# A four-layer convolution and state-space network on one core: the state recurrence of layers 0 and 3 laid out as 8 channels by 16 states per partition block

## The chip, the cores and the metric

The kernel runs on one core of one Trainium2 chip. The metric is the device time of one execution, in microseconds (us); the time before is 17534.35 us, the median of three runs (17520.38 to 17538.02). All data is float32. The engines are TensorE (PE; its weight loads are PEld), VectorE (DVE), ScalarE (ACT), GpSimd (POOL) and SyncE (SP), which issues the transfers.

## The reference, cut to what matters

The input is 4 images of 64 channels by 64 by 64 pixels. Four layers follow one another. Layers 0 and 3 treat an image as a sequence of 4096 tokens and contain a selective state-space recurrence over 128 inner channels with 16 states each:

```
dA  = jnp.exp(dt[..., None] * A)                  # A is (128, 16)
dBx = dt[..., None] * Bm[:, :, None, :] * xc[..., None]
def step(hc, inp):
    dA_t, dBx_t, C_t = inp
    hc = hc * dA_t + dBx_t
    y = jnp.einsum('bds,bs->bd', hc, C_t)
    return (hc, y)
ys = (ys + xc * Dp) * jax.nn.silu(z)
```

dt, xc and z (per channel) and Bm, Cm (per state, the same for all channels) come from projections, a short convolution, silu and softplus. Layer 0 has 3 by 1, 1 by 3 and 1 by 1 convolutions, a ReLU and a layer norm ahead of this and a residual sum behind it; in layer 0 the state starts anew with each image. Layer 3 has a projection, a layer norm, silu and a residual sum behind it, and its state runs on through all four images. Layers 1 and 2 (a selective scan along both image axes, and a 3 by 3 filter with predicted weights) are not changed.

## The kernel before, in words

`Net.__init__` runs setup, then `mambas` for layer 0 of image 0 (tiles named `a`), and for each image layer 1 (`b`), layer 2 (`c`) and a `mambas` call that does layer 3 of this image (`d`) and layer 0 of the next (`a`). Each `mambas` call is a row of **jobs**: an image's 4096 tokens are 8 chunks of 512 tokens, one job each. There are 64 jobs in all, 32 of layer 0 and 32 of layer 3.

Within a job the 128 partitions are the 128 inner channels, and the state index is the loop: `scan` (L401) takes the 16 states in 8 pairs, and each tile of a pair is 128 by 2 by 512. For pair i:

- `spread` (L392) broadcasts two rows of B, and two of C, over the 128 partitions: four matmuls with 32 rows each (a column of the identity as the weights), in four different row blocks of the array, into the PSUM tiles bc0 and bc1 (two banks each).
- `decay` (L405): two ACT exponentials (L408) read dt (`dl`, in SBUF) and make the factors `a`.
- DVE multiplies bc0 by `wx` = dt times xc into `g` (L419, 1024 columns), runs two recurrences of 512 columns (L430, factors `a`, terms `g`, both in SBUF) into `h`, and multiplies bc1 by `h` into `o` (L436, 1024 columns).
- POOL copies the last column of `h` to the state (L433).
- `sums`: two matmuls with the 128 by 128 identity add `o` into the PSUM tile `y`; one more adds D times xc.

The projections and pointwise steps that prepare the next job (`mamba_front`, L455; for layer 0 also `cross`, `relu`, `square`, `norm`, `scaled`, from L584 on) and finish the last one (`out1`, `out2`, ... of `layer0` and `layer3`) are lists of small functions, each with a place. `mambas` sorts them into 17 places, two for each pair, and `scan` calls them between its own instructions. `in_order` (L97) then ties each engine to the order in which the program was written, so an instruction that waits holds up everything written behind it on its engine. On DVE the pieces of a place stand between `g` and the recurrences, or between the recurrences and `o`.

[...] `ps` is shared by all matmuls of `mamba_front`.

Of the kernel before, what the change touches and what calls it, by code (L numbers as in the profile page):

```python
# [10 lines left out]
F32 = mybir.dt.float32  # L11
# [27 lines left out]
SPARE = 512 - UC  # L39

# [14 lines left out]
class Net:  # L55
# [67 lines left out]
    def setup(self, sp, pp):  # L123
# [39 lines left out]

        self.mean64 = self.ctile([C, C], "mean64")
# [30 lines left out]
    def setup_mamba(self, sp, pp, n):  # L195
# [10 lines left out]
        for k in range(4):  # L206
# [15 lines left out]
        m["x4"] = x4 = self.ctile([DIN, 4, 32], f"{n}_x4")  # L222
        nc.vector.memset(x4, 0.0)
        nc.vector.tensor_copy(
            x4[:, :, 0 : NST // 2].rearrange("p (x t) j -> p x t j", t=2),
            xbc.rearrange("p (x j t) -> p x t j", x=2, t=2),
# [124 lines left out]
    def mambas(self, n, b0, b3, x3):  # L351

        nc, tc = self.nc, self.tc
        with ExitStack() as ctx:
            p = {}
            for k, bufs in (("w", 1), ("s", 2), ("n", 2)):
                p[k] = ctx.enter_context(tc.tile_pool(name=f"{n}_{k}", bufs=bufs))
            p["ps"] = ctx.enter_context(tc.tile_pool(name=f"{n}_ps", bufs=1, space=PSUM))
            jobs = self.layer3(b3, x3, p) if b3 is not None else []
            if b0 < NB:  # L360
                jobs += self.layer0(b0, p)
            for job in jobs[0:2]:
                for at, f in job["front"]:
                    if job is jobs[0] or at < 0:
                        f()
            last = {"seen": nc.cur_bb.bb.instructions[-1].name}
            sums = before = None
            self.spread(p, jobs[0], 0, 0)
            for job, after, later in zip(jobs, jobs[1:] + [None], jobs[2:] + [None, None]):
                places = [[] for _ in range(17)]  # L370
                for at, f in after["front"] if after else ():
                    if at >= 0:
                        places[at].append(f)
                for at, f in later["front"] if later else ():
                    if at < 0:
                        places[16 + at].append(f)
                for at, f in before["post"] if before else ():
                    late = before["m"] is self.m3 and after is not None and after["m"] is self.m0
                    places[at + 5 if late and at > 1 else at].append(f)
                sums = self.scan(p, job, after, places, sums, last)  # L380
                before = job
            sums()
            for _, f in before["post"]:
                f()
            if b3 is not None and b0 == NB:
                return
            self.x1 = jobs[-1]["x1"]()

    def spread(self, p, job, x, i):


        ps = p["ps"].tile([DIN, 2, TOK], F32, name=f"{job['n']}_bc{x}{i}", tag=f"bc{x}")  # L392
        for t in range(2):
            r = 64 * x + 32 * t
            pick = self.ident[r : r + 32, r + i : r + i + 1].to_broadcast([32, DIN])
            self.mm(ps[:, t, :], pick, job["bc"][r : r + 32])
        job["ps", x] = ps

    def scan(self, p, job, after, places, sums, last):
        nc, m, n = self.nc, job["m"], job["n"]  # L400
        xc, dl, wx = job["xc"], job["dl"], job["wx"]  # L401
        wide = wx.unsqueeze(1).to_broadcast([DIN, 2, TOK])

        def decay(i):
            a = p["n"].tile([DIN, 2, TOK], F32, name=f"{n}_a{i}", tag="a")  # L405
            for t in range(2):
                j = 2 * i + t
                nc.scalar.activation(a[:, t, :], dl, AF.Exp, scale=m["A"][:, j : j + 1])  # L408
            return a

        a = decay(0)
        for i in range(NST // 2):
            T = lambda tag: p["n"].tile([DIN, 2, TOK], F32, name=f"{n}_{tag}{i}", tag=tag)
            if sums:
                sums()
            if i == 2:
                self.mm(job["y"], m["D"], xc, False, False)
            g, h, o = T("g"), T("h"), T("o")
            nc.vector.tensor_tensor(g, job["ps", 0], wide, ALU.mult)  # L419
            if i + 1 < NST // 2:  # L420
                self.spread(p, job, 0, i + 1)
            elif after:
                self.spread(p, after, 0, 0)
            self.spread(p, job, 1, i)
            now, a = a, decay(i + 1) if i + 1 < NST // 2 else None
            for f in places[2 * i]:
                f()
            for t in range(2):
                st = m["state"][:, 2 * i + t : 2 * i + t + 1]
                nc.vector.tensor_tensor_scan(  # L430
                    h[:, t, :], now[:, t, :], g[:, t, :], st, ALU.mult, ALU.add
                )
            nc.gpsimd.tensor_copy(m["state"][:, 2 * i : 2 * i + 2], h[:, :, TOK - 1])  # L433
            for f in places[2 * i + 1]:
                f()
            nc.vector.tensor_tensor(o, job["ps", 1], h, ALU.mult)  # L436

            def sums(i=i, o=o):

                if i == 0:  # L440
                    job["y"] = p["ps"].tile([DIN, TOK], F32, name=f"{n}_y", tag="y")
                for t in range(2):
                    j = 2 * i + t
                    self.mm(job["y"], self.ident, o[:, t, :], j == 0, j == NST - 1)

            if i == NST // 2 - 1:
                for f in places[16]:
                    f()
            self.in_order(last)
        return sums  # L450

    def mamba_front(self, p, job, src, at):
# [49 lines left out]
        def rows():  # L502
            pr = P("pr")
            self.mm(pr, m["x4"].rearrange("p r j -> p (r j)"), job["xc"])
            job["bc"] = S("bc")
            nc.scalar.copy(job["bc"], pr)
# [12 lines left out]
        def soft4():  # L519
# [7 lines left out]
            zip(at, (conv, conv_out, gate, silu1, silu2, silu3, soft1, rows, soft2, soft3, soft4))  # L527
# [25 lines left out]
    def layer0(self, b, p):  # L553
# [19 lines left out]
        def chunk(c):  # L573
# [8 lines left out]
            def cross(part):  # L582
                def f():
                    if part == 0:  # L584
                        t["px"] = P("px", "ps")
# [21 lines left out]
            def scaled():  # L607
# [7 lines left out]
                (-4, cross(0)), (-2, cross(1)), (0, cross(2)), (0, relu), (1, square), (2, root),  # L615
                (3, newton), (3, scaled),
            ] + self.mamba_front(
                p, job, lambda k: hn[:, t0 + k : t0 + k + TOK], (4, 5, 6, 6, 9, 11, 12, 12, 14, 15, 16)
            )
# [19 lines left out]
            job["post"] = [(1, out1), (2, out2), (3, out3)]  # L639
# [4 lines left out]
    def layer3(self, b, x3, p):  # L644
        nc = self.nc

        def chunk(c):
# [7 lines left out]
                p, job, lambda k: x3[:, t0 + k : t0 + k + TOK], (2, 3, 4, 4, 7, 9, 10, 10, 12, 13, 14)  # L655
# [33 lines left out]
            def silu3():  # L689
# [10 lines left out]
                (1, out1), (2, out2), (3, square), (4, mean),  # L700
                *self.norm(p, n, t, self.l3_pb, None, (5, 7)),
                (7, silu1), (9, silu2), (11, silu3),
# [596 lines left out]
def _layout(i):  # L1299
# [12 lines left out]
    def mamba(n, g, conv_w, conv_b, D):  # L1312
        a[f"{n}_v128"] = c(conv_w, conv_b, g("dt_proj_b"), D, g("A_log"))
# [57 lines left out]
```

## Time and profile before

| | |
|---|---|
| median of three runs | 17534.35 us |
| the profiled execution's own time | 17525.53 us |
| its span, first to last instruction | 17523.8 us |
| mean granted TensorE clock | 0.968 |
| busy: PE / DVE / ACT / POOL | 94% / 92% / 71% / 40% |
| the five `mambas` stretches, by DVE's first and last tile of them | 447, 871, 864, 867, 453 us (3501 us in all) |
| the four layer 1 stretches | 3376 to 3379 us each |
| the four layer 2 stretches | 71 to 72 us each |

The times are in the order of the program, so a change to layers 0 and 3 is read from the five `mambas` stretches, a fifth of the span, and not from the busy shares of the whole, which layer 1 sets. In a group line the columns are source line, engine, operation, output and inputs, shapes and count, then busy time in us and mean ns of one instruction, then idle time of the engine just ahead of it and what ended it. A float32 matmul is recorded as two passes, so a count of 4 stands for two matmuls. Busy time of one group is what no other instruction of the engine covered.

### The profile page before, as it was taken

To read this page: it belongs to the slowest core of one execution; us is meant where nothing else is said; L and a number is where in the kernel's file an instruction comes from. 1 tells how busy PE (TensorE), PEld (TensorE's weight loads), DVE (VectorE), ACT (ScalarE), POOL (GpSimd) and SP (SyncE) were. 2 spreads that over 40 slices of the span, in tenths; PEclk is the share of its full clock that TensorE was granted. 3 is DMA by queue.
4 is the path that set the end of the run, shared out by engine and by line. 5 is a ranking of instruction groups with operands and counts; after the bars stand their busy time and mean duration, and the time that the engine had idled before them with its cause. 6 is when DMAs were issued, how large, how long until landed. Compare 5 with 4: busy or idle time off the path is not lost.

```text
span 17523.8 us, 606527 instructions
## 1 busy us (share of the span) xinstructions
PE 16417.9 (94%) x259788; PEld 10917.5 (62%) x259788; DVE 16093.1 (92%) x18426; ACT 12452.9 (71%) x15787; POOL 7093.0 (40%) x7068
## 2 busy tenths in 40 slices
PE   7999999997899999999779999999977999999997
PEld 2677777762267777776226777777622777777762
DVE  8999999988899999998899999999888999999978
ACT  4688878874468877886447887888644788788864
POOL 0444544441044444445114444444501444444440
PEclk9999999998999999999899999999988999999998
DMA  0233333330033333333003333333200333333320
GB/s 8 76 95 96 96 88 96 94 84 5 1 79 96 96 92 92 95 94 80 5 1 85 96 96 89 94 95 95 75 4 2 90 96 94 89 95 96 96 69 3
DMA packets 580492, 1281.87 MB, mean 73 GB/s; under 512 B 164664, under 2 KB 182304, under 8 KB 577824
## 3 DMA queue, kind: packets, MB, share of 16 engines
q1 hardware_dynamic: 577824, 1243.06, 28.1%
q8 instruction: 2069, 33.90, 0.9%
q14 instruction: 599, 4.91, 0.1%
HBM read 6.64 MB, written 4.19 MB: 1 GB/s over the span
## 4 chain that ended last, share of the span: by engine, by line
PE 85%; DVE 10%; ACT 2%; issue 2%; POOL 0%; DVEq 0%; DMA 0%; SPq 0%; POOLq 0%; ACTq 0%
PE b_u_S L120 24%; PE b_y L120 23%; PE b_z L120 23%; PE b_X L120 5%; PE d_y L120 2%; DVE a_h L430 2%; PE a_y L120 2%; DVE d_h L430 2%; DVE d_o L436 1%; DVE a_o L436 1%; PE c_p L120 1%; PE d_bc L120 1%; DVE a_g L419 1%; PE a_bc L120 1%; PE d_pc L120 1%
## 5 line engine op out<-in xcount | busy, mean ns | idle before, releaser
L1046 ACT ACTIVATE b_k_e<-b_z,shift 128x768 f32<-128x768 f32 x6144 | 5545.3, 903 | 2524.4 <-PE b_z L120 1408.7
L1126 DVE TENSOR_TENSOR b_k_r<-b_u_S,b_k_r 128x768 f32<-128x768 f32 x6144 | 5873.8, 956 | 462.3 <-PE b_u_S L120 110.9
L1101 DVE TENSOR_TENSOR b_k_e<-b_k_e,b_wt 128x768 f32<-128x768 f32 x6144 | 6221.5, 1013 | 29.3 <-ACT b_k_e L1046 29.3
L1046 ACT ACTIVATE b_k_r<-b_z,ln_eps 128x768 f32<-128x768 f32 x6144 | 5505.1, 896 | 0.0
L120 PE MATMUL b_u_S<-b_k_e,b_k_tB 64*64 64x192 f32 x98304 | 5169.8, 325 | 9.3 <-issue 4.3
L120 PEld LDWEIGHTS b_y<-b_k_r,b_k_dC 64*64 64x64 f32 x98304 | 3769.8, 133 | 2246.4 <-issue 2030.8
L120 PE MATMUL b_y<-b_k_r,b_k_dC 64*64 64x192 f32 x98304 | 5123.9, 322 | 36.5 <-DVE b_k_r L1126 36.5
L120 PE MATMUL b_z<-A,b_T 48*64 48x384 f32 x49152 | 5111.8, 485 | 11.6 <-ACT b_k_r L1046 7.9
L1075 POOL TENSOR_TENSOR b_k_tB<-b_BC,tri 128x512 f32<-128x512 f32 x3072 | 3259.7, 1061 | 4086.8 <-PE b_u_S L120 3827.2
L1075 POOL TENSOR_TENSOR b_k_dC<-b_BC,ident 128x512 f32<-128x512 f32 x3072 | 3227.7, 1051 | 2894.2 <-PE b_u_S L120 2015.8
L120 PEld LDWEIGHTS b_u_S<-b_k_e,b_k_tB 64*64 64x64 f32 x98304 | 3670.7, 133 | 581.9 <-issue 229.8
L120 PEld LDWEIGHTS b_z<-A,b_T 48*64 48x64 f32 x49152 | 1867.0, 134 | 203.9 <-ACT b_k_r L1046 48.8
L120 PE MATMUL d_y<-d_o,ident 128*128 128x512 f32 x1024 | 648.8, 767 | 416.3 <-DVE d_o L436 415.9
L120 PE MATMUL a_y<-a_o,ident 128*128 128x512 f32 x1024 | 583.5, 698 | 223.6 <-DVE a_o L436 221.9
L433 POOL COPY l_state<-d_h 128x2 f32<-128x2 f32 x256 | 119.0, 465 | 1625.5 <-DVE d_h L430 1625.5
L120 PEld LDWEIGHTS d_y<-d_o,ident 128*128 128x128 f32 x1024 | 212.3, 230 | 811.8 <-DVE d_o L436 617.6
L433 POOL COPY l_state<-a_h 128x2 f32<-128x2 f32 x256 | 110.5, 432 | 1425.5 <-DVE a_h L430 1425.5
L430 DVE TENSOR_TENSOR_SCAN a_h<-a_a,l_state,a_g 128x512 f32<-128x512 f32 x512 | 629.4, 1271 | 29.8 <-ACT a_u L497 0.5
L430 DVE TENSOR_TENSOR_SCAN d_h<-d_a,l_state,d_g 128x512 f32<-128x512 f32 x512 | 629.0, 1269 | 26.9 <-DVE d_g L419 1.4
L408 ACT ACTIVATE d_a<-d_dl,l_A 128x512 f32<-128x512 f32 x512 | 339.2, 711 | 354.5 <-DVE d_dl L522 183.2
L408 ACT ACTIVATE a_a<-a_dl,l_A 128x512 f32<-128x512 f32 x512 | 336.0, 709 | 318.4 <-DVE a_h L430 159.9
L120 PEld LDWEIGHTS a_y<-a_o,ident 128*128 128x128 f32 x1024 | 192.3, 208 | 593.1 <-DVE a_o L436 375.6
(352 smaller groups left out, 9914.4 us busy)
## 6 DMA issues: line engine op xcount, KB each, us to landing
b_k_r<-b_k_r SPq DMA_DIRECT2D x6144, 192.0 KB, 3.0
b_xs<-x SPq DMA_DIRECT2D x128, 67.0 KB, 2.7
b_xs<-x SPq DMA_DIRECT2D x128, 66.8 KB, 2.3
b_BC<-b_BC SPq DMA_DIRECT2D x512, 12.0 KB, 2.1
xin<-in_x SPq DMA_DIRECT2D x16, 256.0 KB, 5.8
out<-d_so SPq DMA_DIRECT2D x32, 128.0 KB, 2.3
l1w_cw<-in_l1w_cw SPq DMA_DIRECT2D x1, 384.0 KB, 3.4
l1h_cw<-in_l1h_cw SPq DMA_DIRECT2D x1, 384.0 KB
```

Source lines behind the costliest of these rows:

```text
L120: self.nc.tensor.matmul(out, lhsT=lhsT, rhs=rhs, start=start, stop=stop)
L408: nc.scalar.activation(a[:, t, :], dl, AF.Exp, scale=m["A"][:, j : j + 1])
L419: nc.vector.tensor_tensor(g, job["ps", 0], wide, ALU.mult)
L430: nc.vector.tensor_tensor_scan(h[:, t, :], now[:, t, :], g[:, t, :], st, ALU.mult, ALU.add)
L433: nc.gpsimd.tensor_copy(m["state"][:, 2 * i : 2 * i + 2], h[:, :, TOK - 1])
L436: nc.vector.tensor_tensor(o, job["ps", 1], h, ALU.mult)
L1046: nc.scalar.activation(o.rearrange("p x (j c) -> p j x c", j=2), zin, AF.Sigmoid, bias=bias, scale=scale)
L1075: nc.gpsimd.tensor_tensor(out, m.unsqueeze(3).to_broadcast(shape), x.unsqueeze(1).unsqueeze(2).to_broadcast(shape), ALU.mult,)
L1101: nc.vector.tensor_tensor(e, e, chunks[q]["w"][:, i, :].unsqueeze(1).unsqueeze(2).to_broadcast([128, 2, 2, D1]), ALU.mult,)
L1126: nc.vector.tensor_tensor(r, S.pop(k)[:, :, 0:UC], r, ALU.mult)
```

## The change: what it does

The layout of the recurrence is turned. A **group** is now 8 channels by 16 states on the 128 partitions, and a job is 16 groups (`NG`) of 512 columns, one recurrence each.

- B and C are made for all 128 partitions once in each job: `rows(0)` and `rows(1)` multiply xc by weights `wbc` in which the 16 columns are repeated 8 times, and ACT copies the results to SBUF tiles `bc0` and `bc1`.
- `decay`: a matmul with 32 rows (`pick`) spreads the 8 channels of dt that belong to the group over 128 partitions, into one PSUM bank `pe`; ACT takes the exponential from PSUM, with a scale for each partition, into `a` (5 buffers). It runs 4 groups ahead (`EXPS`).
- `wide`: the same for `wx`, into a PSUM tile `g` with 3 buffers, 3 groups ahead (`WXS`).
- `drive`: DVE multiplies `g` by `bc0` in place, in PSUM, one group ahead of the recurrence.
- `state`: the recurrence, terms from PSUM.
- `weigh`: after each second group POOL copies the last columns to the state and multiplies the pair's `h` (128 by 1024, 3 buffers) by `bc1`, in place, in SBUF.
- `sums`: two matmuls of 128 rows and 32 columns each (`gather`) sum the pair's states, each into another block of 32 partitions of `y`, one pair after `weigh`. D times xc now starts `y`.
- The pieces of the jobs beside it get 16 places, one for each group (`AT`); the layer 0 pieces `cross` to `scaled` move from places -4 to 3 to places -8 to -2. `px` moves from `ps` to the bank of `pv`. PSUM is `pe` 1, `g` 3, `y`, `ps`, `pl`, `pv` 1 each.
- Setup makes `gather`, `of32` and `wbc`; each `mambas` call makes `pick` with one DVE copy. The load of `v128` has the same size, with A permuted.

The core of the diff:

```diff
+GS = 8
+NG = DIN // GS
+EXPS, WXS = 4, 3
+AT = -1, 0, 1, 1, 4, 5, 6, 7, 7, 8, 9, 10
...
+            for j in range(EXPS):
+                self.decay(p, *steps[j])
+            for j in range(WXS):
+                self.wide(p, *steps[j])
+            self.drive(*steps[0])
...
+                for f in places[k]:
+                    f()
+                if j + 1 < len(steps):
+                    self.drive(*steps[j + 1])
+                self.state(p, job, k)
+                if j + EXPS < len(steps):
+                    self.decay(p, *steps[j + EXPS])
+                if j + WXS < len(steps):
+                    self.wide(p, *steps[j + WXS])
+                if k % 2:
+                    self.weigh(job, k - 1)
+                    if j > 2:
+                        self.sums(p, *steps[j - 3])
+                self.in_order(last)
...
+    def spread(self, p, out, x, k):
+        r = slice(32 * (k % 4), 32 * (k % 4) + 32)
+        self.mm(out, p["pick"][r, k // 4].rearrange("p c n -> p (c n)"), x[r])
+
+    def decay(self, p, job, k):
+        n = f"{job['n']}_{k}"
+        ps = p["ps"].tile([DIN, TOK], F32, name=f"{n}_pe", tag="pe")
+        self.spread(p, ps, job["dl"], k)
+        a = job["a", k] = p["n"].tile([DIN, TOK], F32, name=f"{n}_a", tag="a", bufs=EXPS + 1)
+        self.nc.scalar.activation(a, ps, AF.Exp, scale=job["m"]["A"][:, k : k + 1])
+
+    def drive(self, job, k):
+        g = job["g", k]
+        self.nc.vector.tensor_tensor(g, job["bc", 0], g, ALU.mult)
+
+    def state(self, p, job, k):
...
+        self.nc.vector.tensor_tensor_scan(
+            h[:, t, :], job.pop(("a", k)), job.pop(("g", k)), m["state"][:, k : k + 1],
+            ALU.mult, ALU.add,
+        )
+
+    def weigh(self, job, k):
+        nc, h = self.nc, job["h", k]
+        nc.gpsimd.tensor_copy(job["m"]["state"][:, k : k + 2], h[:, :, TOK - 1])
+        nc.gpsimd.tensor_tensor(
+            h, job["bc", 1].unsqueeze(1).to_broadcast([DIN, 2, TOK]), h, ALU.mult
+        )
+
+    def sums(self, p, job, k):
+        if k == 0:
+            job["y"] = p["ps"].tile([DIN, TOK], F32, name=f"{job['n']}_y", tag="y")
+            self.mm(job["y"], job["m"]["D"], job["xc"], True, False)
+        h = job.pop(("h", k))
         for t in range(2):
+            q, g = (k + t) % 4, (k + t) // 4
+            self.mm(
+                job["y"][32 * q : 32 * q + 32], self.gather[:, g, :], h[:, t, :], False, g == 3
+            )
...
-                (-4, cross(0)), (-2, cross(1)), (0, cross(2)), (0, relu), (1, square), (2, root),
-                (3, newton), (3, scaled),
+                (-8, cross(0)), (-7, cross(1)), (-6, cross(2)), (-6, relu), (-5, square), (-4, root),
+                (-3, newton), (-2, scaled),
```

## The prediction

> **What bounds it now.** The page's first part gives shares of the whole span:
>
> ```profile
> PE 16417.9 (94%) x259788; PEld 10917.5 (62%) x259788; DVE 16093.1 (92%) x18426; ACT 12452.9 (71%) x15787; POOL 7093.0 (40%) x7068
> ```
>
> Layer 1 makes these. The change lives in the `mambas` stretches, so I cut three pieces there, from one `yz` (the end of a job) to a later one: 6 layer 0 jobs of the first stretch, 7 layer 3 jobs, 7 layer 0 jobs behind them.
>
> ```profile
> core 0: us, PE busy (x) PEld busy (x) DVE busy (x) ACT busy (x) POOL busy (x), PEclk, DMA share, GB/s
> 143.00:452.40 309.40, 246.96 (x758) 76.24 (x758) 285.12 (x272) 146.94 (x216) 33.11 (x57) 0.96 0.00 0
> 4058.40:4437.50 379.10, 282.77 (x843) 88.82 (x844) 337.38 (x326) 187.06 (x279) 35.39 (x63) 0.88 0.01 3
> 4437.50:4814.30 376.80, 306.58 (x890) 92.14 (x888) 335.19 (x321) 177.35 (x261) 38.11 (x67) 0.91 0.00 1
> ```
>
> A job takes 309.4/6 = 51.6, 379.1/7 = 54.2 and 376.8/7 = 53.8 us. With the later stretches cut the same way the means are 53.0 (layer 0) and 54.2 (layer 3). DVE is busy 89 to 92%: it is the bound, and ACT (50%) and POOL (10%) are nearly free. PE is second, 75 to 81% busy. The groups say what DVE does, and the two c rows are used below:
>
> ```profile
> L430 DVE TENSOR_TENSOR_SCAN d_h<-d_a,l_state,d_g 128x512 f32<-128x512 f32 x512 | 629.0, 1269 | 26.9 <-DVE d_g L419 1.4 <-ACT d_dv L496 0.5
> ...
> L408 ACT ACTIVATE d_a<-d_dl,l_A 128x512 f32<-128x512 f32 x512 | 339.2, 711 | 354.5 <-DVE d_dl L522 183.2 <-DVE d_h L430 171.3
> ...
> L436 DVE TENSOR_TENSOR d_o<-d_bc,d_h 128x1024 f32<-128x1024 f32 x256 | 311.6, 1217 | 136.2 <-PE d_bc L120 132.7
> ...
> L419 DVE TENSOR_TENSOR d_g<-d_bc,d_wx 128x1024 f32<-128x1024 f32 x256 | 310.3, 1212 | 0.4
> ...
> L1279 POOL TENSOR_TENSOR c_acc<-c_acc,c_m 128x512 f32<-128x512 f32 x128 | 162.2, 1267 | 123.0 <-DVE c_m L1277 111.3 <-DVE c_st L1247 3.5
> ...
> L1277 DVE TENSOR_TENSOR c_m<-c_pk,x 128x512 f32<-128x512 f32 x144 | 97.0, 680 | 30.3 <-POOL c_acc L1279 14.4 <-POOL x L1283 7.9 <-PE c_pk L120 6.4
> ```
>
> The 132.7 us before `d_o` are DVE waiting for the C rows: PE reaches them late. The order of PE in one layer 3 job shows why:
>
> ```profile
> 4237.29 1.98 PE L120 MATMUL d_y<-d_o,ident 128*128 128x512 f32 x4
> 4239.20 1.14 PE L120 MATMUL d_bc<-d_bc,ident 32*128 32x512 f32 x8
> 4245.54 3.78 PE L120 MATMUL d_y<-d_o,ident 128*128 128x512 f32 x4 [5.20 <-DVE d_o L436]
> ```
>
> Two full matmuls take 1.98 us; four of 32 rows, in different row blocks, 1.14 together. After 5.2 us of waiting the same two take 3.78: the granted clock is halved (mean 0.88 in that window).
>
> **DVE's sum.** In the DVE timeline of that job a pair takes 1.14 (`o`, start to next start) + 1.35 (`g`, and the gap to the recurrence that depends on it) + 2.46 (two recurrences) = 4.95 us, eight times 39.6. The change removes `o` (1.14) and `g` (1.35) and adds two `drive`s of 512 columns. No row writes PSUM from DVE; the nearest (L1277, PSUM times SBUF) lasts 0.68 and starts every 0.60 when free, the dearest 512-column row is 0.74 (L549). I take 0.60, as each `drive` stands one group ahead of its recurrence and the gap goes. The recurrence with its terms in PSUM is not shown either; from SBUF it is 1.23 in a row of two, and the 1024-column rows cost the same from PSUM as from SBUF, so I keep 1.23. A group is 1.83, a job 16 x 1.83 = 29.3. The pieces beside it stay on DVE: 10.0 us in layer 0 (two of 1024 columns, 1.22 and 1.20; eleven of 512 at about 0.69), 10.7 in layer 3. DVE's floor is 39.3 and 40.0 us, against 39.6 + 10 or 10.7 before: 10.3 us freed in each job. What is late next takes half back.
>
> **The product on POOL.** 1024 columns cost between 2 x 1.05 (L1075, 512 columns, both inputs repeated) and 2 x 1.27 (L1279): I take 2.4, plus 0.2 to 0.45 for the state copy, eight times 22 us of a job: it fits. But POOL and DVE get in each other's way. First DVE, then POOL, in one stretch of layer 2:
>
> ```profile
> 8281.93 0.23 DVE L1243 TENSOR_TENSOR c_wl<-c_p,l_b 128x72 f32<-128x72 f32 x1 [0.69 <-PE c_p L120]
> ...
> 8283.50 0.77 DVE L1248 TENSOR_TENSOR c_wl<-c_wl,c_st 128x72 f32<-128x72 f32 x1
> ```
>
> ```profile
> 8282.91 2.62 POOL L1279 TENSOR_TENSOR c_acc<-c_acc,c_m 128x512 f32<-128x512 f32 x2 [0.25 <-DVE c_st L1247]
> ```
>
> 72 columns take 0.23 with an input from PSUM and 0.77 with both in SBUF, ending where POOL's first product ends. `c_m` (one input from PSUM) is not held. So `drive` should run free, and the pieces with both inputs in SBUF wait for a running product. A product starts behind each odd group and lasts until 2.9 us after its recurrence (0.1 + 0.4 + 2.4). An even group with no such piece takes DVE 1.83, so a piece that opens the next odd place waits 1.1: places 5 and 9. At place 10 four such pieces in a row let the copy and then the product in between: 0.2 + 2.4. Layer 0's norm pays 0.4 more. Sum: 5.2 us (layer 0), 4.8 (layer 3).
>
> The recurrence keeps one SBUF stream, `a`. The trace has no recurrence beside a POOL product for longer than 0.08 us (then 1284 ns against 1270), so its cost lies between 0 and 2.4 us a pair; I take 0, by `c_m`.
>
> [...]
>
> **PE.** Before, a pair costs 1.91 + 1.07 (start to next start) = 2.98. After: four spreads, two at a time in different row blocks, and two sums in different column blocks. Nothing shows sums of 32 columns; between side by side (1.07, as `d_bc`) and in turn (1.91, as `d_y`) I take 1.07, because the 64 by 64 blocks of layer 1 also run four at a time. That is 3.1 to 3.2 a pair, 43 us a layer 0 job with 17.7 of pieces, 36 in layer 3: below DVE, but with little room. PE is in order: `decay`'s spread waits until ACT has read the single bank `pe`, and the `wide` that the next `drive` needs is queued behind it. `wide` leads by one group beyond the one in hand, so the four matmuls of `conv` (3.63 us) at place 15 hold `drive` up by about 2.5. The sums wait for POOL, with 3.7 us and a spread to hide its 2.9: nothing.
>
> **ACT.** An exponential from PSUM is 0.69 (as L468, 687 ns), and spread and exponential alternate: about 1.9 a group, hidden by four groups of lead. But `silu3` (place 5) to `soft2` (place 7) is 1.2 of matmul, five ACT pieces of 0.64, and two exponentials: 5.8 us, where DVE has two groups, 3.7. DVE waits 2.0. Before, the same pieces stood three half pairs apart (7.4 us) and were covered.
>
> **Sum.** Layer 0: 39.3 + 5.2 + 2.5 + 2.0 = 49.0 against 53.0. Layer 3: 40.0 + 4.8 + 2.5 + 2.0 = 49.3 against 54.2. 32 x (4.0 + 4.9) = 285 us saved. Each of five stretches starts dearer: the first `wide` stands behind four spreads and three exponentials in turn, about 7 us, and setup adds 3: 38. Transfers are unchanged. 285 - 38 = 247 off the profiled execution's 17525.5 is 17278; the median lies 9 above it: **17287 us**, with 17120 to 17440 by the bounds of these costs.
>
> **Rivals**, from the same median.
> - Covers hold: POOL and DVE interleave well and the lead hides `conv` and the silu chain; jobs of 44.5. 32 x (8.5 + 9.7) - 38 = 544: **16990**. For it: the pieces wait only if they meet a product. Against: PE's 43 us.
> - The sums run in turn: 8 x 0.86 = 6.9 more on PE, 50 us a layer 0 job, 53 with the waits, 50 in layer 3: 32 x (0 + 4.2) - 38 = 96: **17440**; lower clocks would make it no change.
> - **Slower: the recurrence can't run beside POOL's product.** Place: the two recurrences of each pair; price 2.4 a pair: 8 x (3.66 + 2.4) + 10 = 58.5 and 59.2. 32 x (5.5 + 5.0) + 38 = 374: **17910**. It decides from about 1.1 us of waiting a pair. For it: `a` and the state come from SBUF. Against: `c_m`.
>
> **Chances.** Forecast 0.50; covers hold 0.18; sums in turn 0.17 (half of it below 17440, a third of it within 0.2% of no change, a little slower); recurrence held 0.12; else 0.03. A measurement of this kernel tells 0.2% (35 us) from no change. Faster 0.77, same 0.07, slower 0.16. The range, 16970 to 17580, takes in all but the held recurrence and the best covers.
>
> **What would show it.** Right: no `o` on DVE, `drive` near 0.68 and recurrence near 1.27; products of 2.4 on POOL; `silu3`, `soft3` and `soft4` two to four times as long as before; DVE waiting for PE before `drive` around place 15; sums starting within 0.1 us of each other. Wrong: recurrences beyond 1.5 us, products beyond 3, PE's clock below 0.85, or DVE waiting for ACT's factors at most groups.

## The result, and the profile after

The changed kernel takes **18906.56 us** (median of 4 runs, 18904.84 to 18912.01) against 17532.79 beside it: ratio **1.0785**, 95% interval 1.0766 to 1.0804. The prediction was 17287 with a range up to 17580, so it was wrong in sign and by 1620 us. The profiled execution took 18907.0 (span 18905.3).

All of it lies in the five `mambas` stretches: together 3501 us before and 4922 now, cut by DVE's first and last instruction in each (46 us of the growth is only that this first instruction now stands earlier). Layer 1 (3379 us a time) and layer 2 (71) are as they were. A layer 3 job takes 71.6 us instead of 54.2 (82 to 87 where its neighbours belong to layer 0), a layer 0 job mostly 74 to 79 instead of 53.

Of the page of the changed kernel, the engines' line and the rows of PE and of its clock:

```profile
PE 18224.0 (96%) x259916; PEld 11069.6 (59%) x259916; DVE 15720.0 (83%) x18436; ACT 12481.3 (66%) x15851; POOL 8275.7 (44%) x7580
...
PE   8999999999999999999999999999999999999998
...
PEclk7799999985589999998558999999855899999985
```

DVE's busy time fell by 373 us, as the change meant it to. PE's rose by 1806 with 128 more instructions among 260 thousand, so each one got longer; and where the stretches lie, the clock row says 5 to 8 tenths while the PE row says 9. The windows, cut from one `yz` to a later one, of five layer 0 jobs of the first stretch, five layer 3 jobs, and two layer 0 jobs behind them:

```profile
core 0: us, PE busy (x) PEld busy (x) DVE busy (x) ACT busy (x) POOL busy (x), PEclk, DMA share, GB/s
188.90:574.30 385.40, 363.20 (x650) 83.73 (x650) 208.24 (x225) 125.36 (x186) 119.05 (x88) 0.60 0.00 0
4280.30:4641.30 361.00, 330.94 (x590) 75.65 (x590) 211.33 (x231) 133.77 (x202) 119.13 (x85) 0.57 0.01 2
4977.20:5134.90 157.70, 150.57 (x260) 34.45 (x260) 83.42 (x91) 50.47 (x76) 46.01 (x34) 0.56 0.00 0
```

PE is the bound: 92 to 95% busy at a mean clock of 0.56 to 0.60 (before 0.88 to 0.96 at 75 to 81%). DVE is 53 to 59% busy. The trace records the granted clock as either full or half (1.0 in half of the entries and 0.5 in the others: 352 before, 218 now), in stretches that are multiples of 3.413 us; of the five `mambas` stretches, 776 of 3501 us were at half before, 4110 of 4922 are now. The record begins only 98.8 us into the span before and 140.7 us after. The matmuls of 512 columns ahead of that last 1.06 us in the median, as at half clock (0.59 and more at full), so some 49 and 106 us of the first stretch are missing from these two sums.

The groups of the layer 3 window show that the durations of single instructions on DVE, ACT and POOL are close to what the prediction took:

```profile
L124 PE MATMUL d_pe<-d_dl,d_pick 32*128 32x512 f32 x161 | 152.0, 1040 | 23.7 <-ACT d_a L442 23.7
L124 PE MATMUL d_g<-d_wx,d_pick 32*128 32x512 f32 x160 | 151.7, 1045 | 2.2 <-DVE d_h L460 2.2
L460 DVE TENSOR_TENSOR_SCAN d_h<-d_a,l_state,d_g 128x512 f32<-128x512 f32 x80 | 101.7, 1272 | 0.0
L469 POOL TENSOR_TENSOR d_h<-d_bc,d_h 128x1024 f32<-128x1024 f32 x40 | 96.0, 2399 | 3.3 <-POOL l_state L468 0.2
L124 PE MATMUL d_y<-d_h,gather 128*32 128x512 f32 x162 | 72.3, 988 | 0.0
L453 DVE TENSOR_TENSOR d_g<-d_bc,d_g 128x512 f32<-128x512 f32 x81 | 55.6, 687 | 66.6 <-PE d_g L124 66.6
L442 ACT ACTIVATE d_a<-d_pe,l_A 128x512 f32<-128x512 f32 x81 | 55.5, 685 | 206.3 <-PE d_g L124 189.7 <-PE d_pe L124 16.6
```

`drive` (L453) lasts 687 ns, the recurrence (L460) 1272, the product on POOL (L469) 2399. But `drive` waited 66.6 us for PE, the exponential (L442) 206. In the timeline of one job:

```profile
4336.12 7.19 PE L124 MATMUL d_pc<-x,l_wk 64*128 64x512 f32 x8
...
4343.24 1.22 PE L124 MATMUL d_pe<-d_dl,d_pick 32*128 32x512 f32 x1
...
4343.25 1.22 PE L124 MATMUL d_g<-d_wx,d_pick 32*128 32x512 f32 x1
...
4345.24 1.92 PE L124 MATMUL d_y<-d_h,gather 128*32 128x512 f32 x4
...
4345.39 0.70 DVE L453 TENSOR_TENSOR d_g<-d_bc,d_g 128x512 f32<-128x512 f32 x1 [7.25 <-PE d_g L124]
```

The four matmuls of `conv` take 7.19 us (3.70 at full clock before, 3.63 to the next start). One `decay` and one `wide` spread run together, from 4343.24 to 4345.24; two sums side by side take 1.92 (1.05 where the clock is full). A pair of groups has two such couples of spreads and one of sums: 2 x 2.0 + 1.86 = 5.86 us, eight times 46.9. In the third window above, added up from each matmul's start to the next (1.3 us at most for one), the spreads and sums of a layer 0 job take 48.7 us, the matmuls of its pieces 27.4, and the other 2.7 of its 78.8 us are waiting.

### The profile page after: what moved, and what is told of

It reads as the page before. It is cut to its first block, busy times and chain, and to the rows that moved or that the text cites. A ratio compares the mean times of both kernels' runs of the same rounds, so it can differ in the third digit from the quotient of the medians.

```text
span 18905.3 us, 607797 instructions
## 1 busy us (share of the span) xinstructions
PE 18224.0 (96%) x259916; PEld 11069.6 (59%) x259916; DVE 15720.0 (83%) x18436; ACT 12481.3 (66%) x15851; POOL 8275.7 (44%) x7580
## 5 line engine op out<-in xcount | busy, mean ns | idle before, releaser
L442 ACT ACTIVATE a_a<-a_pe,l_A 128x512 f32<-128x512 f32 x512 | 351.2, 686 | 1410.7 <-PE a_g L124 1151.2
L442 ACT ACTIVATE d_a<-d_pe,l_A 128x512 f32<-128x512 f32 x512 | 350.7, 685 | 1336.8 <-PE d_g L124 1180.1
L124 PE MATMUL d_pe<-d_dl,d_pick 32*128 32x512 f32 x1024 | 965.5, 1040 | 156.5 <-ACT d_a L442 156.5
L124 PE MATMUL d_g<-d_wx,d_pick 32*128 32x512 f32 x1024 | 956.1, 1047 | 12.1 <-DVE d_h L460 12.1
L124 PE MATMUL a_pe<-a_dl,d_pick 32*128 32x512 f32 x768 | 709.4, 1019 | 63.7 <-ACT a_a L442 63.7
L468 POOL COPY l_state<-a_h 128x2 f32<-128x2 f32 x256 | 63.5, 248 | 1609.5 <-DVE a_h L460 1552.5
L124 PEld LDWEIGHTS d_pe<-d_dl,d_pick 32*128 32x128 f32 x1024 | 233.9, 282 | 891.6 <-ACT d_a L442 418.5
L453 DVE TENSOR_TENSOR d_g<-d_bc,d_g 128x512 f32<-128x512 f32 x512 | 351.1, 687 | 466.8 <-PE d_g L124 466.8
L453 DVE TENSOR_TENSOR a_g<-a_bc,a_g 128x512 f32<-128x512 f32 x512 | 351.1, 686 | 463.6 <-PE a_g L124 463.4
```

The costliest lines, as they stand in the source:

```text
L124: self.nc.tensor.matmul(out, lhsT=lhsT, rhs=rhs, start=start, stop=stop)
L442: self.nc.scalar.activation(a, ps, AF.Exp, scale=job["m"]["A"][:, k : k + 1])
L453: self.nc.vector.tensor_tensor(g, job["bc", 0], g, ALU.mult)
L468: nc.gpsimd.tensor_copy(job["m"]["state"][:, k : k + 2], h[:, :, TOK - 1])
```

## The experiments

The theories. **A**: PE's clock is halved because the new matmuls use too little of the array. **B**: POOL's product holds up DVE. **P**: PE works in the order of the program (`in_order`), and the single bank of `decay` with what is queued behind it stops it. Most variants were run once, with a profile, beside one to seven runs of the kernel before on the same chip (medians 17511.7 to 17528.8); variants run four times spread over 2 to 25 us. Half clock means the sum over the five stretches in the trace's record. There are 64 jobs, 32 of each layer, and some of the expectations multiply by half of that: in the run with useless products 27 us a job make 1728 us, not 860; the waits for POOL's product that the prediction priced (the expectations call them locks) are 320 us in all, not 160; and the sums for the product on DVE and for the last two runs double as well. The order is that of the argument.

**POOL's product left out.**
```
-            h, job["bc", 1].unsqueeze(1).to_broadcast([DIN, 2, TOK]), h, ALU.mult
+            h[:, :, 0:1], job["bc", 1][:, 0:1].unsqueeze(1).to_broadcast([DIN, 2, 1]),
+            h[:, :, 0:1], ALU.mult
```

> This kernel leaves out POOL's product with C but for its first column: the sums add the bare states, everything else of the changed kernel stays. Theory A (PE is the bound because its clock is halved; the clock gate goes by how much of the array works, and matmuls of 32 rows or 32 columns use a quarter each): the clock stays at 0.56 to 0.62 in the jobs and the time within 1.5% of the changed kernel, 18650 to 19000 us. Theory B (POOL's products hold DVE's SBUF pieces and the sums, and PE idles behind them): 8 to 12 us off each of 64 jobs, 18150 to 18400 us.

18881.46 us, half clock 4100 us. Its window at the place of the changed kernel's five layer 3 jobs:

```profile
4280.30:4641.30 361.00, 329.68 (x594) 74.99 (x592) 200.67 (x234) 133.85 (x201) 30.57 (x87) 0.57 0.01 2
```

POOL's busy time went from 119 to 31 us, and PE's busy time and clock in it stay the same. B falls as the cause.

**Sums of 128 columns**, zeros but for 8: as many matmuls, wider, no longer side by side.
```
...
-            self.mm(job["y"][32 * q : 32 * q + 32], self.gather[:, g, :], h[:, t, :], False, g == 3)
+            c = DIN - GS - 32 * ((k + t) % 4) - GS * ((k + t) // 4)
+            self.mm(job["y"], p["gather"][:, c : c + DIN], h[:, t, :], False, k + t == NG - 1)
```


> The two sums of a pair get weights of 128 columns (zeros but for 8), so each fills the array and they run in turn: more work for PE, 0.86 us a pair at full clock, 1.7 at half. Theory A: full passes lift the clock above 0.9 in the jobs; a layer 0 job takes 50 to 55 us instead of 78.8, in all 17300 to 17800 us. Rival C (PE's clock falls because PE waits in order for ACT, POOL and DVE, whatever the width): the clock stays near 0.6 and a job grows by 8 x 1.7 = 13.6 us, in all 19600 to 19800 us.

18321.06 us, half clock 1569: 585 us faster, though two sums now take 1.98 us of PE at full clock, where two side by side take 1.05. The sign speaks for A; the size is half of what was expected, as jobs still take mostly 60 to 71 us.

**Spreads of 64 rows and sums of 64 columns**, padded with zeros; the groups are taken in block order 0, 2, 1, 3 so that neighbours still run side by side.
```
+BLOCK = 0, 2, 1, 3
...
-        r = slice(32 * (k % 4), 32 * (k % 4) + 32)
-        self.mm(out, p["pick"][r, k // 4].rearrange("p c n -> p (c n)"), x[r])
+        q = BLOCK[k % 4]
+        r = slice(64 * (q // 2), 64 * (q // 2) + 64)
+        self.mm(out, p["pick"][r, k // 4, q % 2], x[r])
...
+            y = job["y"][64 * (q // 2) : 64 * (q // 2) + 64]
+            self.mm(y, p["gather"][:, 4 * (q % 2) + g, :], h[:, t, :], False, k + t >= NG - 2)
```


> The same number of matmuls, side by side in the same twos, but spreads of 64 rows and sums of 64 columns (weights padded with zeros; the four blocks of channels are taken in the order 0, 2, 1, 3, so that each two take both halves of the array). Theory A: every visit of the recurrence's matmuls fills the array, the clock goes above 0.9, and what the prediction worked out for DVE, POOL and ACT at full clock comes back: jobs of 48 to 53 us, 17200 to 17550 us. Rival C: no change, 18800 to 19000 us.

18062.13 us (18041.77 to 18066.95; ratio to before 1.0305, 1.0287 to 1.0322), half clock 1598: much of the loss is gone, but not the 17200 to 17550 expected.

**Spreads of 64 rows alone** (the first three changed lines; sums as in the changed kernel).

> Spreads of 64 rows as in the kernel with both, sums left at 32 columns. Theory A: four of six visits fill the array, two use half; mean area while busy about 0.85 of what it is with both, so most of the clock comes back: above 0.85, jobs of 49 to 56 us, 17250 to 17750 us. Rival C: no change, 18800 to 19000 us.

17994.17 us, half clock 1484: **912 us of the loss undone** by padding a matmul's rows with zeros. 17250 to 17750 had been expected; part of what was left is P, below.

**Sums of 64 columns alone** (the last lines; spreads of 32 rows).

> The changed kernel with sums of 64 columns (zeros beside the 8 of each group's channels), its spreads left at 32 rows: the other half of the run in which both were 64. If the clock follows the area that a matmul occupies, rows and columns alike, half of a wider sum counts as half of a wider spread: there are two sums to four spreads in a pair, so about half of the 912 us of the wide spreads, 18350 to 18600. If only the rows count (a sum has all 128 of them already), nothing: 18850 to 18950.

18981.56 us, half clock 4237: no gain, 75 us lost. The order of the groups is changed here too (0, 2, 1, 3), so that order is not what helped. So wider **rows** brought the gain here (half clock 4110 to 1484 us), and wider columns brought none (4110 to 4237). The windows of five layer 3 jobs, first with 64 rows in the spreads, then with 64 columns in the sums:

```profile
4162.30:4435.70 273.40, 228.12 (x590) 60.75 (x590) 210.48 (x231) 133.84 (x201) 119.35 (x85) 0.86 0.01 3
```

```profile
4306.40:4681.60 375.20, 359.64 (x591) 86.33 (x590) 211.29 (x230) 133.89 (x201) 119.31 (x85) 0.53 0.01 2
```

With the same count of instructions, but for one or two, the one runs at 0.86, the other is 96% busy at 0.53. It corrects theory A (I had counted area), and fits the 128 columns: the sums, all of whose rows are in use, then ran one after the other and so for longer (the 1.98 us).

With rows as the measure I went through the windows of 3.413 us of the stretches in all twenty kernels (22,418 windows, nearly all that the clock's record covers): the share of the array's rows in use at each instant (matmuls in different row blocks add up, sums side by side count once), averaged over the window, against the clock of the next window. Each matmul instruction of 512 columns counts for 0.43 us at full clock and 0.85 at half, the spacing of those in a row. The share is therefore an estimate: with its details the counts shift by some per cent, most in the rows next to the two limits.

| mean share of rows in use | half now: full next | full now: full next |
|---|---|---|
| below 0.36 | 0 of 1297 | 27 of 2746 |
| 0.36 to 0.40 | 0 of 387 | 412 of 737 |
| 0.40 to 0.60 | 1 of 2738 | 3072 of 3107 |
| 0.60 to 0.75 | 166 of 2821 | all 3711 |
| 0.75 to 0.80 | 508 of 585 | all 787 |
| above 0.80 | all 2337 | all 1165 |

In these windows the counts turn near **0.75 up** and **0.38 down**: of those at half clock, 167 of 7243 below 0.75 were followed by full clock and 2845 of 2922 above it; of those at full clock, 27 of 2746 below 0.36 stayed there and 8735 of 8770 above 0.40. PE's time in use, whatever the rows, does not part them: of 2677 windows at half clock in which matmuls, by the same spacings, ran for at least 90% of the time, 1062 were followed by full clock. For a pair of groups, from the durations above (spreads two at a time 1.07 us a couple at full clock, 2.0 at half; sums 1.05 and 1.86; about 5.2 us a pair where DVE sets the pace), the pieces left out:

| kernel | at full clock | at half clock |
|---|---|---|
| before (spreads four at a time, two full sums) | (1.07 + 1.91) / 5 = 0.60 | above 0.75 |
| after | (2.14 x 0.5 + 1.05) / 5.2 = 0.41 | (4.0 x 0.5 + 1.86) / 5.86 = **0.66** |
| spreads of 64 rows | (2.14 + 1.05) / 5.2 = 0.61 | all rows while busy |

By this estimate the changed kernel's 0.41 at full clock lies just above where the counts turn down, so that a little waiting takes it there, and its 0.66 at half clock lies below where they turn up, although PE is 92 to 95% busy: of its 1052 windows at half clock and below 0.75, none was followed by full clock.

**Useless full products.** Two zero-weight matmuls of 128 by 128 into y, in seven of eight pairs.
```
+        for _ in range(2 if k < NG - 2 else 0):
+            self.mm(job["y"], p["nil"], job["xc"], False, False)
```


> The changed kernel with two more matmuls of 128 by 128 in each pair of groups (seven pairs a job), whose weights are zeros: they add nothing to y and nothing else is altered. At half clock a full one lasted 1.9 us, so if PE's clock stayed as it is, or if PE were simply too busy, a job would grow by 14 x 1.9 = 27 us: 32 x 27 = 860 us on top of 18906, about 19770. Theory A (the clock follows how much of the array the matmuls occupy, so that narrow ones starve it): with two full matmuls a pair, as before the change, the clock comes back, PE needs 8 x 2.1 + 14 x 0.95 + 18 + 8 = 56 us in a layer 0 job and 48 in layer 3, and the time falls below 18300 although work was added; half clock from 4110 us to below 1700.

18462.56 us, half clock 1266: more work, 444 us less time, where a clock that stayed would have cost 1728 more. The clock came back as expected; the time did not fall below 18300, since PE now has that work to do (294 of 328 us busy in five layer 3 jobs, clock 0.86).

**P: the order on PE.** From the run with 64 rows, three edits: the wide spread written ahead of the decay spread; two banks for `pe` (the bank `pl` given up, its users moved to `ps`); both.
```
-        ps = p["ps"].tile([DIN, TOK], F32, name=f"{n}_pe", tag="pe")
+        ps = p["ps"].tile([DIN, TOK], F32, name=f"{n}_pe", tag="pe", bufs=2)
```


> On the kernel with spreads of 64 rows (17994 us): in each step the spread for the term is written ahead of the spread for the factor, nothing else. Theory D (what is left of the loss is order: the factor's spread waits for ACT to empty the single bank, ACT is behind the pieces of other jobs, and the term that DVE needs next is queued behind that spread): 100 to 300 us off, 17700 to 17900 us. Rival E (PE's own work at a clock near 0.8 is the bound): within 50 us of 17994.

17907.07, 87 us less.

> On the kernel with spreads of 64 rows: the factors' spread gets two PSUM banks instead of one. For that the bank of the two norm inputs goes: layer 0's moves to the bank of the front matmuls, layer 3's too, with one more ACT copy of 0.6 us a layer 3 job. Theory D: PE no longer stops at each factor for ACT; 200 to 500 us off, 17500 to 17800 us, layer 3 jobs near 50 us and layer 0 jobs below 58. Rival E: within 60 us of 17994.

17849.29, 145 us less.

> 64 rows, two banks for the decay spreads, and the wide spread written first: the two edits that gave 145 and 87 us one by one. If the two waits are different ones, both together give 232: 17760. If they are one wait in PE's order, no more than the larger: about 17850. I expect 17760 to 17860.

17784.9, 209 us less: nearly the sum, so mostly two waits. The two banks in the changed kernel itself, with 32 rows:

> The changed kernel with its 32 rows, and two PSUM banks for the decay spreads, as in the run of 64 rows that gained 145 us by them. Theory A (at half clock PE is full, so its order matters little): within 18750 to 18950. Theory P (the single bank and the order on PE carry the loss): at least 145 us less, below 18750.

18749.58, 157 us less, half clock 3780: on the border between the two ranges, but the gain is no smaller than the 145 us with 64 rows. So my forecast that the order matters little at half clock was wrong: the bank is worth about as much at either width. P is a second, smaller cause.

**Sums of four groups together**, from the run with two banks.
```
-                    if j > 2:
-                        self.sums(p, *steps[j - 3])
+                    if j > 4 and k % 4 == 1:
+                        self.sums(p, *steps[j - 5])
```


> On the kernel with two banks: the sums of four groups are issued together, 32 columns each in the four column blocks, once in two pairs (one more buffer for the states). Full array in each such visit, and PE saves about 1 us in four groups at full clock, 4 us a job. Theory A (the gate goes by the share of the array in use): the clock rises further; with E, PE's bound falls: 100 to 300 us less than the kernel with two banks. If neither PE nor its clock binds there any more: within 50 us of it.

17968.01: 119 us *more*, half clock up from 1318 to 1724. The count of rows would fit, if four sums side by side take the time of two; that is the expectation's estimate, and no row shown here measures it. Whether the clock makes all of the 119 us was not tested; the sums also come later.

**One useless full product a pair**, on the run with two banks and the wide spread first.

> The same as the run with both edits on PE's order, with one more matmul of 128 by 128 with zero weights in each pair (seven a job). At full clock it costs PE 0.95 us, 6.7 a job. Theory A: half clock (about 1300 us of the stretches) falls below 900, and layer 0 jobs from 64 to 69 down to below 60, although PE has more to do; 17500 to 17750. If the layer 0 jobs are bound by PE's work and not by its clock, they grow by 3 to 7 us: 17850 to 18000.

17959.11, 174 us more, although half clock fell from 1148 to 886. Layer 0 jobs went from 61.5 to 65 us, within the 3 to 7 us named: there PE's work and order, not the clock alone, set the pace.

**POOL's product again, now that PE is faster.** Left out in the run with 64 rows:

> The kernel with spreads of 64 rows, with POOL's product left out but for its first column (the sums add the bare states): the price of the product once PE runs faster. The prediction's term (DVE's SBUF pieces wait 4.8 to 5.2 us a job for running products) makes 200 to 330 us less than 17994. If PE's order hides these waits: less than 80 us.

17793.89, 200 us less. Left out in the run with both order edits:

> The run with 64 rows, two banks and the wide spread first, with the product only in the first column of each group (it leaves out the product with C elsewhere; PE, ACT and the order of everything stay). What POOL's product costs through locks and lateness once PE is faster. My prediction priced the locks at 4.8 to 5.2 us a job, 160 us in all: 17500 to 17640 from 17785. If the rest of the loss is PE's, less than 60 us go.

17662.47, 122 us less. And moved to DVE (`nc.gpsimd` to `nc.vector`):

> The same run with the product on DVE instead of POOL (one instruction of 1024 columns, about 1.15 us, for each pair; nothing left out). DVE gets 8 x 1.15 = 9.2 us more a job, and loses the locks, which the page prices at 5 to 6 us a job. If DVE has room (it waited for PE and ACT in a sixth of the time), the time stays within 17700 to 17850; if DVE is the bound, 32 x 4 = 130 us more: 17850 to 17950. Should it fall below 17529, it would beat both kernels.

17885.62, 101 us more than on POOL. So over 64 jobs the product costs 1.9 to 3.1 us a job through the waits of DVE's pieces and through lateness (in the changed kernel, where PE is the bound, 0.4), and on DVE it costs 1.6 more. The 122 us lie between the two forecasts: the waits are there, at less than half of the 320 us they were priced at.

**Spreads four at a time.** If rows in use at one time count, four spreads of 32 rows in four row blocks serve as well as wide ones, and take half of PE's time: by the durations above 1.07 us for four, as in the kernel before, where two couples take 2.14. For that the two `drive`s of a pair stand ahead of its first recurrence, and the factors get one more buffer:
```
+                if k % 2 == 0:
+                    self.drive(*steps[j])
                     self.drive(*steps[j + 1])
                 self.state(p, job, k)
+                if k % 2 == 0:
+                    self.wides(p, steps[j + 2 : j + 4])
+                    for step in steps[j + EXPS : j + EXPS + 2]:
+                        self.decay(p, *step)
...
```


> 32 rows and two banks, as in the run that took 18750, but the spreads go out four at a time, in four different row blocks (two wide, two decay, behind the first recurrence of each pair), so that all rows are in use while they run, and PE's work is not widened. By the records so far, a window of 3.4 us of half clock is followed by full clock where the share of rows in use, times the time, is at least 0.75, and one of full clock by half clock where it is below 0.38. If rows at one time are what counts, half clock falls from 3780 us to below 1500 and the time below 18000, without any wider matmul; a job's PE work falls to 8 x 2.1 + 18 = 35 us in layer 0, so that 17450 to 17850 is likely. If it is the width of each matmul that counts, about 18750 again, less at most 300 for the shorter PE work.

**17581.37 us** with 32 rows: 1168 less than the run with two banks, which differs in this and in what goes with it, and 66 above the kernel before (17515.32). Five layer 3 jobs of that run with two banks, for comparison:

```profile
4254.20:4610.70 356.50, 326.04 (x591) 76.91 (x591) 210.42 (x231) 134.68 (x206) 119.18 (x85) 0.59 0.01 2
```

In the timeline of the run with four at a time, the spreads start two by two within 0.02 us and run together:

```profile
4165.54 0.70 PE L124 MATMUL d_g<-d_wx,d_pick 32*128 32x512 f32 x2
4165.55 0.70 PE L124 MATMUL d_pe<-d_dl,d_pick 32*128 32x512 f32 x2
4166.07 0.59 PE L124 MATMUL d_g<-d_wx,d_pick 32*128 32x512 f32 x2
4166.09 0.59 PE L124 MATMUL d_pe<-d_dl,d_pick 32*128 32x512 f32 x2
```

Half clock is 1658 of 3597 us, above the 1500 that I had set: at 0.41 a pair, (1.07 + 1.05) / 5.2, the clock still drops, but it comes back, to a mean of 0.84 and 0.76 where it was 0.59. The windows of four layer 3 jobs and of four of layer 0:

```profile
4120.30:4312.30 192.00, 156.01 (x473) 38.40 (x474) 164.87 (x185) 105.04 (x164) 95.30 (x68) 0.84 0.01 3
4604.90:4837.50 232.60, 202.52 (x521) 47.39 (x522) 162.42 (x180) 97.58 (x148) 95.89 (x69) 0.76 0.00 0
```

In these four a layer 3 job takes **48.0 us** (54.2 before), in the others one of layer 0 58.2 (53.0 before). With the three jobs behind the four (53.9, 58.3 and 60.7 us, the last two beside layer 0's pieces) the mean of a stretch's seven layer 3 intervals is 52.1. DVE's waits in the layer 3 stretch (us in total, times, longest) are led by the end of each job:

```profile
DVE d_yz L697 <- PE d_y L124: 37.7, 6, 11.2
```

In the layer 0 window DVE waits 48.6 us in 5 such waits.

**Two tries at the rest.** The sums ahead of the pieces of their place, and the end of a job one place later:
```
+                if k % 2 and j > 2:
+                    self.sums(p, *steps[j - 3])
                 for f in places[k]:
...
-            job["post"] = [(2, out1), (3, out2), (4, out3)]
+            job["post"] = [(3, out1), (4, out2), (5, out3)]
```


> The run of four spreads at a time, with two moves in the order: the sums stand ahead of the pieces of their place on PE (so the last sums of a job stand ahead of part of the next job's), and the end of a job (yz, its projection and what follows) one place later. There DVE waited 6 to 9 us a job for y. If these waits are real losses, 2 to 4 us a job: 17450 to 17530 from 17581. If PE's work at half clock only moves, within 50 us of 17581.

17731.32 (ratio to before 1.0122, 1.0107 to 1.0137): 150 us more. The waits for y are no longer among DVE's large ones, but half clock rose to 2028 us and layer 3 jobs to 58. Why this order lowers the clock was not taken apart further. (The forecast of 2 to 4 us a job would be 128 to 256 us over 64 jobs; the sign is wrong either way.) With layer 0's five taps as three matmuls as well (the input a second time in partitions 64 to 127, shifted by a row and a column):
```
-            taps = ((0, 1, 1), (1, 0, 1), (2, 2, 1), (3, 1, 0), (4, 1, 2))
+            taps = ((0, 1, 1), (1, 0, 1), (2, 1, 2))
+            nc.sync.dma_start(xin[C:, r : r + 16, 2 : W + 2], self.a["x"][b, :, r : r + 16, :])
```


> The same, and layer 0's cross of five taps as three matmuls: one of 64 rows and two of 128 (a second copy of the input, shifted by a row and a column, lies in partitions 64 to 127). Four instructions less a layer 0 job and all rows in use in four of six: 1.7 us of PE at full clock, 3.4 at half, and more full clock. 16 jobs of 1.5 to 4 us: 25 to 65 us below the run without it; below 17515 it beats both kernels.

17757.43 (1.0136, 1.0119 to 1.0153), no gain either; half clock 2225, of which 58 us lie ahead of the point where the record of the run without them begins. None of the versions beats the kernel before.

## Why the prediction was wrong, point by point

- **What failed: the step on PE**, "That is 3.1 to 3.2 a pair, 43 us a layer 0 job with 17.7 of pieces, 36 in layer 3: below DVE, but with little room." The count of matmuls and the pairing were right (two sums side by side 1.05 where the clock is full, against 1.07 taken; of layer 1's 64 by 64 matmuls, the reason given, four start within 0.02 us of each other in the trace of before, as at 2000.53). The durations were taken at full clock; at half they are 5.86 a pair, and a layer 0 job takes 76 us of PE (48.7 + 27.4). The prediction shows a halved clock further up (3.78 us where 1.98 was usual), puts it beside a wait, and does not ask what the change does to the clock. The trace of before could have told: of its windows at half clock, all 135 with a share of rows above 0.75 were followed by full clock, and 2 of 59 below it; and the changed spreads, two instead of four at a time, use half of the rows. Undoing that alone (64 rows) gives back 912 us; four at a time, on top of the second bank, 1168.
- **The order on PE**, "hidden by four groups of lead": wrong as well, by 209 us with 64 rows, 157 with 32 for the bank alone. PE waited 23.7 us for ACT ahead of the `decay` spreads in the layer 3 window, and what is queued behind them waits too, so the lead of four groups is not there. The wait of `drive` behind `conv`, priced at 2.5 us a job, was 7.25 in the job shown above. The 2.0 us for ACT's chain were not measured by themselves.
- **DVE's sum** was right: `drive` 0.69, recurrence 1.27, `o` gone. Where PE lets it (four layer 3 jobs with four spreads at a time), DVE is busy 164.87 / 4 = 41.2 us a job, the waits for POOL's product included, against a floor of 40.0 without them, and a job takes 48.0 against 49.3 forecast. That the two lie so close is partly luck: the waits for POOL's product were priced too high, and those for `y` at a job's end, 6.3 us on average there, were put at nothing.
- **The product on POOL** was right in its duration (2.4 us forecast, 2.40 measured). The two-SBUF pieces wait for it as said. In one job of the changed kernel, DVE's pieces and then POOL's products:

```profile
4310.62 2.27 DVE L552 SCALAR_TENSOR_TENSOR d_dl<-d_dl,d_u 128x512 f32<-128x512 f32 x2
...
4316.62 2.72 DVE L559 TENSOR_TENSOR d_wx<-d_dl,d_sl 128x512 f32<-128x512 f32 x1
```

```profile
4309.27 2.35 POOL L469 TENSOR_TENSOR d_h<-d_bc,d_h 128x1024 f32<-128x1024 f32 x1
...
4315.98 2.80 POOL L469 TENSOR_TENSOR d_h<-d_bc,d_h 128x1024 f32<-128x1024 f32 x1
```

  Two pieces that would last 1.3 together, and one of 0.7, end 1.3 and 0.6 us after the product that ran when they started. The price was too high: 5.2 and 4.8 us a job are 32 x 10.0 = 320 us in all, where leaving the product out gained 122 to 200 once PE was faster, and 25 in the changed kernel.
- **The rival "the recurrence can't run beside POOL's product"** fell: in the changed kernel 199 recurrences with at least 1.2 us of a product beside them took 1269 ns, 659 with none 1271. It was the only rival priced on the slower side, and it stood on the wrong engine; the 0.12 on it were no cover for the clock.
- **The rival "sums in turn"** fell too: two of them take 1.05 us side by side at full clock (1.98 in turn, in the run with 128 columns), and in the count of rows above they count once, so that this adds nothing to the share. Its "lower clocks would make it no change" is the one price that the prediction sets on the clock: the 96 us between this rival and no change.
- **The layer 0 forecast of 49.0** was reached by no version, the ends of the stretches aside, where fewer jobs are left to prepare. The best in a row were 54.7 (the sums ahead of the pieces) and 58 (four spreads at a time); which part of that is half clock (0.76 in the latter), which the order of the pieces, stays open. The product hardly counts in it: left out or on DVE, layer 0 jobs stay at 61 to 62 us in the run with both order edits.
- **The sign to look for** was named: "PE's clock below 0.85". It is 0.57.

## What to carry to other kernels

Before narrowing matmuls, work out, from durations in a trace, for a window of 3.4 us what share of the array's rows is in use, at full and at half clock: here a change that saved PE no time but halved the rows that the spreads use at a time took its mean clock from between 0.88 and 0.96 to between 0.56 and 0.60, and 92 to 95% busy did not protect from it. Several narrow matmuls at a time in different row blocks (1168 us), or rows padded with zeros (912 us), gave most of the loss back without one more matmul; wider columns did not (75 us lost), and with sums in four instead of two column blocks half clock rose from 1318 to 1724 us. And an engine forecast at nearly the bound's own time needs its durations at its worst clock in the sum, not in the list of signs: a layer 0 job took 76 us of PE where 43 were forecast.

## What the runs showed of the hardware that was not expected

- In these stretches the granted clock of TensorE went with the share of rows in use, as estimated above over 22,418 windows of 3.413 us: of those at half clock, 2845 of 2922 above 0.75 were followed by full clock and 167 of 7243 below it; of those at full clock, 27 of 2746 below 0.36 stayed there and 8735 of 8770 above 0.40. Busy time was not enough: PE at 92 to 95% busy stayed at a mean clock of 0.56 to 0.60. Nor did wider columns raise it: half clock was 4237 us with sums of 64 columns, 4110 with 32.
- Zero weights raised the clock too: half clock fell from 4110 us to 1484 with spreads padded with zeros (912 us gained) and to 1266 with zero-weight products (444 us gained).
- A recurrence on DVE with its factors in SBUF and its terms in PSUM was not held by POOL's product (1269 ns beside one, 1271 without), while pieces with both inputs in SBUF were (2.72 us in the job shown, 0.69 in the kernel before).
